# Where pieces of other work go beside an attention stream: a planner's rules and charges changed

## The chip, the cores and the metric

The kernel runs on one core of a Trainium2 chip. It uses all engines of that core: TensorE (PE in the profile) multiplies matrices, ScalarE (ACT) computes exponentials and tanh, VectorE (DVE) and GpSimd (POOL) do elementwise work, and SyncE (SP) issues most of the DMAs. The metric is the device time of one execution in microseconds. A single profiled execution gives the trace from which durations are read.

## The reference, cut to what matters

The input x has 4 images of 64 x 64 pixels with 128 channels, so 4096 tokens of 128 numbers in each of 4 batches. Two layers follow each other.

- Layer 0: ELU, two 3x3 convolutions, a gate `a * sigmoid(b)`, then causal attention with one head (queries and keys of 4 numbers, values of 16), whose result goes through W3 and is added to the gate's output and to x.
- Layer 1: a layer norm, attention with 16 heads of 8 numbers over all 4096 tokens of the image, a gated feed-forward network of 344 hidden units, another layer norm, and a mixture of 8 experts of which each token uses two.

```
scores = jnp.einsum('bqhd,bkhd->bhqk', q, k)        # 16 heads, 4096 x 4096 each
probs = jax.nn.softmax(scores.astype(jnp.float32), axis=-1)
attn = jnp.einsum('bhqk,bkhd->bqhd', probs, v)
h = x + attn @ wo
ffn = jax.nn.silu(h @ w1) * (h @ w3) @ w2
...
router_probs = jax.nn.softmax(x @ router_w + router_b, axis=-1)
top_p, top_i = jax.lax.top_k(router_probs, 2)
```

The 16-head attention dominates: 4 x 16 x 4096 x 4096 exponentials.

## The kernel before, in words

**The stream.** The 16-head attention of layer 1 is one long stream of rounds. Its unit is a segment: four heads (a group), 512 queries (a chunk) and all 32 key tiles of 128 keys. For one key tile a round does the following. TensorE computes the scores of the four heads into two PSUM tiles named `s` (four matmuls, each on 32 rows of the array), ScalarE takes the exponential of each `s` tile (128 x 1024) into a tile `e`, and TensorE later multiplies `e` with the values, summing into the PSUM tile `acc`. There are three `s` tiles, so TensorE can't compute scores much ahead of ScalarE. The value products trail the scores by a few rounds; they are kept in a list `undone` and issued in quarters of 128 queries (`add_values`).

**VectorE's tile.** In every full segment, key tile 20 isn't given to ScalarE. Class `Beside` gives its exponentials to VectorE: four units (one per head) each compute scores into the PSUM bank `m`, and VectorE evaluates a polynomial with nine instructions per unit (tiles `ey`, `em`, `eg`). When all four are done, two value halves (`half`, `acc<-ey` in the profile) add the tile to `acc`. The planner keeps its own estimate of when VectorE is done, `done_at`, and `can()` allows a half only when that time has come. Halves not placed by a segment's last value product are forced in there (`beside_rest`). So a segment has 31 rounds.

**Pieces.** All other work (the convolutions, the first attention's operands, the second attention's operands of the next batch, and the last part: output projection, feed-forward, router and experts of the batch at hand) is written as Python generators in the list `fillers`. Each `yield` ends a piece and names what it is taken to cost TensorE (mostly 0.46). Most pieces write into the one PSUM bank `m`, which VectorE then reads; `bank_held` says that a piece isn't finished with it, and `empty` that the bank is expected to be free. A round of the first attention (`first_step`) is put into the stream in the same way as a round of the second.

**The planner.** What is written in which place is decided while the program is built, in the `while True` loop at the end of `fast_path` (from line 1494). The order on every engine is the order as written (`InOrder`, L114 in the profile, which is why all instructions have that line). In each round the loop adds `EXPS` to a clock `turn_at`, writes one step's scores, and then has an account `left`: what is over of `EXPS` after the scores (`SCORES`) and the value quarters that must be done now (`VALUES` each), plus up to `AHEAD` from the round before. From this account it places, in this order: a piece that was held to go on, the jobs of VectorE's tile (`HEAD` for a unit, `PIECE` for a half), up to two pieces (`PIECE` each), and what value quarters still fit. `left` can be overdrawn: a job does so when it is late by its own list of due rounds, and a piece when the credit is high. The credit grows by `rate` per round (the work that is left divided by the rounds that are left, at least 40), shrinks by what is placed, and is at most 3.0. In batches 0 to 2 the pieces are the last parts of the batch and the preparation of the next one; in batch 3 they are only last parts. What isn't placed when the stream ends runs alone after it (`run_alone`).

Of the kernel before, what the change touches and what calls it, by code (L numbers as in the profile page):

```python
# [21 lines left out]
NQ = N // QB  # L22
# [5 lines left out]
NSLOT = P // SLOT  # L28
# [98 lines left out]
def fast_path(ctx: ExitStack, tc: tile.TileContext, a: dict, where: dict, out: bass.AP, verdict):  # L127
# [158 lines left out]
    steps_in, undone, fillers = [], [], []  # L286
    bank_held = [False]

    def do_step(step):
        scores, values, split = step  # L290
        undone.append([values, scores(), 4, split])

    def add_values(quarters):

        while quarters > 0:
            values, es, left, split = undone[0]
            some = min(left, quarters) if split else left
            values(es, *((4 - left, 4 - left + some) if split else ()))
            quarters -= some
            undone[0][2] -= some  # L300
            if some == left:
                undone.pop(0)

    def behind():
        return sum(step[2] for step in undone)

    def finish(leave):
        add_values(sum(step[2] for step in undone[: max(0, len(undone) - leave)]))
# [10 lines left out]
    def insert():  # L319

        while fillers:
            r = advance(fillers[0])
            if r is not None:
                return r[0]
            fillers.pop(0)
        return 0.0
# [510 lines left out]
    def second_operands_beside(b, st):  # L837

        while st.second < NQ:
            while len(st.ready) <= st.second or not folded[0]:  # L840
                if not alone[0]:
                    return
                yield 0.0, "wait"
            yield from second_operands(b, st)
# [208 lines left out]
    def beside_work(until, beside_pool=True):  # L1053
        while beside_todo and dve_at[0] + beside_todo[0][0] <= until:
            if not beside_pool and max(dve_at[0], turn_at[0] + 0.5) < pool_at[0]:
                break
            beside_todo.pop(0)[1]()
# [206 lines left out]
    batches = []  # L1264

    def run_alone(gens, until):

        gens, last = list(gens), {}
        while gens and not (until() and "rounds" not in last.values()):
            for gen in list(gens):  # L1270
                r = next(gen, None)
                while r is not None and r[1] == "held":
                    r = next(gen, None)
                last[gen] = r and r[1]
                if r is None:
                    gens.remove(gen)
                if steps_in:
                    do_step(steps_in.pop(0))
                    finish(1)
                elif undone:  # L1280
                    finish(0)
        while steps_in:
            do_step(steps_in.pop(0))
        finish(0)
        return gens
# [101 lines left out]
    now, quiet = [0], [False]  # L1387
# [75 lines left out]
    def fold_and_spread():  # L1463

        yield from spread(dve, taps1, wino1)
        pw = bank()
        pe.matmul(pw[:, :C], lhsT=once[:, :P], rhs=w3c[:, :C], start=True, stop=True)
        dve.tensor_copy(w3f[:, :C], pw[:, :C])
        pool.tensor_copy(w3f[:, C:], k_of["slot_row"])
        folded[0] = True  # L1470
        yield 0.0, "stop"
        yield from spread(dve, taps2a, wino2[:, :, :C], 0.5)

    def spread_beside():
        yield from spread(pool, taps2b, wino2[:, :, C:])
# [4 lines left out]
    left = run_alone(  # L1480
        [st.conv, first_attention(0, st), second_operands_beside(0, st), fold_and_spread(), spread_beside()],
        lambda: st.second >= plan[0].n and len(spread_of) == 3 and not st.plain,
    )
# [5 lines left out]
    credit, waiting = 0.0, False  # L1489


    EXPS, SCORES, VALUES, PIECE, HEAD, AHEAD = 1.81, 0.54, 0.218, 0.446, 0.23, 0.2
    ahead = 0.0
    while True:
        turn_at[0] += EXPS
        if steps_in:
            do_step(steps_in.pop(0))
        else:
            step = next(steps, False)
            if step is False:  # L1500
                break
            waiting = step is None
            if waiting:
                finish(0)
            else:
                do_step(step)
        b = now[0]
        if batches[b].second == NQ and len(batches) == b + 1 and b + 1 < B:
            Batch(b + 1)
            begun = 0  # L1510
            while begun < len(fillers) and (fillers[begun][2] in fetching or fillers[begun][2] is None):
                begun += 1
            fillers.insert(begun, [first_attention(b + 1, batches[b + 1]), PREPARE, None, False])

        rate = 1.0
        if batches[b].second == NQ:
            later = PREPARE * (B - len(batches)) + LAST * (last_parts_left[0] - 1)
            rate = (sum(part[1] for part in fillers) + later) / max(40, sum(steps_left) - 160)
        credit = min(3.0, credit + rate)
        must = max(0, behind() - 8)  # L1520
        left = ahead + EXPS - SCORES - VALUES * must
        took, beside = None, False
        if not quiet[0] and fillers and fillers[0][3] and not waiting:
            took = insert()
            credit -= took
            left -= took
        empty = bank_held[0] or bank_at[0] <= turn_at[0] + 0.3 or batches[b].second < NQ
        for job in jobs:
            cost = HEAD if job.units < NSLOT else PIECE
            if job.can() and empty and (left >= cost or job.late()):  # L1530
                if not (quiet[0] or bank_held[0] or steps_in or waiting):
                    job.piece()
                    left -= cost
                    beside = True
        for n in range(1 if waiting else 2):
            if took is None:
                go = waiting or not (quiet[0] or beside) and empty and credit > 0.0
                go = go and (waiting or left >= PIECE or credit > 1.5)
            else:
                go = took > 0.0 and bank_held[0] and left >= PIECE  # L1540
            if not go:
                break
            shift[0] = 0.0 if took is None else took
            took = insert()
            shift[0] = 0.0
            credit -= took
            left -= took
        add_values(must)
        while left >= VALUES and behind() > 6 and undone[0][3] and undone[0][3]():
            add_values(1)  # L1550
            left -= VALUES
        ahead = min(max(left, 0.0), AHEAD)
        for job in jobs:
            job.step()
        beside_work(turn_at[0] + 2.9, any(job.age > 3 * job.units + 4 for job in jobs if job.halves < 2))
# [681 lines left out]
def conv_attn_hybrid_kernel(tc: tile.TileContext, a: dict, where: dict, out: bass.AP):  # L2237
    nc = tc.nc
    with tc.tile_pool(name="verdict", bufs=1) as pool:
        verdict = pool.tile([1, 1], FP, name="verdict")  # L2240
        fast_path(tc, a, where, out, verdict)

        beyond = nc.values_load(verdict.bitcast(mybir.dt.int32))
        with tc.If(beyond > 0x3F800000):
            general_path(tc, a, where, out)
# [30 lines left out]
```

## Time and profile before

| what | us |
|---|---|
| median of 4 runs (7977.22 to 7985.18) | 7980.22 |
| the profiled execution, its own time | 7972.5 |
| its span, first to last instruction | 7970.7 |
| TensorE busy | 7755.9 (97%) |
| ScalarE busy | 7662.6 (96%) |
| VectorE busy | 4799.6 (60%) |
| 8256 exponentials `e<-s`, busy together | 7600.9 |
| ScalarE's longest wait in sum, `e` for `s` | 101.8 |

The stream begins at about 180 us, when the first layer of the first batch has gone far enough; 4123 of its rounds are written by the loop. By the start times of the exponentials batch 0 runs to about 2240 us, batch 1 to 4155, batch 2 to 6074 and batch 3 to 7914. After 7914 us the last part of the last chunk runs alone.

"Busy" of TensorE is a union of overlapping, modelled durations; it doesn't say that TensorE works at its peak. An idle time in a group's line is the time the engine stood still just before its instructions, with what ended it. A wait too short to leave an idle gap between overlapping instructions isn't in that column. Such a wait shows only in the distances between start times.

### The profile page before, as it was taken

The page shows a single profiled execution, that of the slowest core. Times are in us where ns is not written, and L with a number is a line of the kernel's source. Part 1 is how long each engine was busy: PE and PEld are TensorE (multiplying, and loading weights), DVE is VectorE, ACT ScalarE, POOL GpSimd, SP SyncE. Part 2 cuts the span into 40 slices and gives each one's busy share as a digit, 9 for nine tenths or more (in the row PEclk, how much of TensorE's full clock was granted, in tenths as well). Part 3 has the DMA queues.
Part 4 walks back from the last instruction along what each step waited for, and adds up shares of the span by engine and source line. Part 5 has one row for each costly group of instructions (what it writes and reads, how often), then busy time and mean ns, then how long its engine had stood idle before and what let it go on. Part 6 is the DMA issues. An engine that isn't in the chain of part 4 may idle for free.

```text
span 7970.7 us, 237947 instructions
## 1 busy us (share of the span) xinstructions
PE 7755.9 (97%) x103701; PEld 3277.6 (41%) x103701; DVE 4799.6 (60%) x9289; ACT 7662.6 (96%) x8459; POOL 671.6 (8%) x592
## 2 busy tenths in 40 slices
PE   7899999999999999999999999999999999999998
PEld 3333444444444444444444444444444333333334
DVE  4333556462666776666666777666666666666664
ACT  1899999999999999999999999999999999999996
POOL 1201211000022100000001210000000000000000
PEclk9999999999999999999999999999999999999998
DMA  2222011111110111111010011111111111111221
GB/s 73 67 68 69 23 61 33 61 40 53 35 34 15 50 39 52 38 29 43 25 41 29 19 43 43 51 42 35 32 29 53 50 49 52 51 54 50 70 73 38
DMA packets 334834, 360.96 MB, mean 45 GB/s; under 512 B 148211, under 2 KB 224467, under 8 KB 333779
## 3 DMA queue, kind: packets, MB, share of 16 engines
q1 hardware_dynamic: 329763, 343.87, 13.9%
q8 instruction: 814, 13.34, 0.7%
q10 hardware_dynamic: 4016, 1.77, 0.1%
q14 instruction: 241, 1.97, 0.1%
HBM read 209.50 MB, written 136.05 MB: 43 GB/s over the span
## 4 chain that ended last, share of the span: by engine, by line
PE 43%; issue 3%; DVE 2%; ACT 2%; DMA 0%; POOL 0%; SPq 0%; ACTq 0%; DVEq 0%; POOLq 0%
PE acc L114 22%; PE s L114 12%; PE m L114 9%; ACT e L114 1%; DVE ey L114 1%; DVE h L114 0%; DVE em L114 0%; DVE t L114 0%; DVE eg L114 0%; DVE by_e L114 0%; SPq L114 0%; DMA blocks<-d_y 0%; POOL rs L114 0%; POOL v L114 0%; POOL xt L114 0%
## 5 line engine op out<-in xcount | busy, mean ns | idle before, releaser
L114 ACT ACTIVATE e<-s 128x1024 f32<-128x1024 f32 x8256 | 7600.9, 1112 | 106.7 <-PE s L114 101.8
L114 PE MATMUL acc<-e,vg 128*9 128x128 f32 (+3 forms) x61880 | 4277.0, 387 | 1.9 <-DVE at L114 1.8
L114 PE MATMUL s<-qx,f_kx 32*128 32x512 f32 (+1 forms) x16512 | 2554.6, 496 | 86.4 <-ACT e L114 56.5
L114 PEld LDWEIGHTS acc<-e,vg 128*9 128x9 f32 x61880 | 1561.2, 90 | 1776.6 <-issue 1208.3
L114 PEld LDWEIGHTS s<-qx,f_kx 32*128 32x128 f32 (+1 forms) x16512 | 1048.1, 182 | 2066.5 <-ACT e L114 1338.7
L114 DVE SCALAR_TENSOR_TENSOR ey<-ey,eg 128x512 f32<-128x512 f32 x1344 | 941.0, 700 | 31.9
L114 DVE COPY at<-acc 128x512 f32<-128x512 f32 x131 | 90.6, 691 | 594.9 <-PE acc L114 590.5
L114 PE MATMUL m<-v,f_wino 128*32 128x256 f32 x5376 | 420.3, 391 | 12.1 <-POOL v L114 7.3
L114 DVE TENSOR_SCALAR ey<-m 128x512 f32<-128x512 f32 x448 | 307.7, 687 | 89.6 <-PE m L114 79.8
L114 DVE SCALAR_TENSOR_TENSOR eg<-em,ey 128x512 f32<-128x512 f32 x448 | 316.8, 707 | 11.4
L114 DVE SCALAR_TENSOR_TENSOR ey<-ey,em 128x512 f32<-128x512 f32 x448 | 316.7, 707 | 9.6
L114 POOL TENSOR_TENSOR rs<-ve,f_minus_half 128x4 f32<-128x4 f32 x64 | 65.3, 1020 | 3028.8 <-DVE ve L114 3028.8
L114 DVE SCALAR_TENSOR_TENSOR ey<-eg 128x512 f32<-128x512 f32 x448 | 312.9, 698 | 0.0
L114 POOL TENSOR_TENSOR v<-r 128x1024 f32<-128x1024 f32 x112 | 219.1, 1962 | 971.0 <-PE m L114 970.5
L114 DVE COPY sd<-m 128x512 f32<-128x512 f32 x168 | 116.0, 691 | 301.4 <-PE m L114 301.0
L114 PE MATMUL m<-f_we,y2T 128*32 128x256 f32 x3968 | 291.9, 388 | 0.0
L114 DVE TENSOR_TENSOR by_e<-m,gates 128x512 f32<-128x512 f32 x248 | 170.3, 687 | 176.6 <-PE m L114 175.4
L114 PE MATMUL m<-hT,f_fw 128*32 128x256 f32 (+1 forms) x2728 | 233.0, 390 | 1.3 <-DVE hT L114 1.1
L114 POOL TENSOR_TENSOR t<-t,h 128x512 f32<-128x512 f32 x32 | 44.5, 1391 | 2240.8 <-DVE h L114 2240.8
L114 DVE TENSOR_TENSOR t<-m,t 128x512 f32<-128x512 f32 x61 | 42.2, 692 | 308.8 <-PE m L114 308.7
L114 DVE TENSOR_SCALAR em<-ey 128x512 f32<-128x512 f32 x448 | 200.5, 447 | 13.7
L114 DVE TENSOR_SCALAR em<-em 128x512 int32<-128x512 int32 x448 | 196.2, 438 | 10.0
(260 smaller groups left out, 4380.0 us busy)
## 6 DMA issues: line engine op xcount, KB each, us to landing
f_kx<-d_k SPq DMA_DIRECT2D x139, 512.0 KB
qx<-d_q SPq DMA_DIRECT2D x152, 256.0 KB
d_q<-two SPq DMA_DIRECT2D x64, 512.0 KB
d_a<-at SPq DMA_DIRECT2D x128, 256.0 KB
vg<-d_v SPq DMA_DIRECT2D x32, 576.0 KB
d_k<-two SPq DMA_DIRECT2D x32, 512.0 KB
d_v<-vc SPq DMA_DIRECT2D x32, 288.0 KB
xe<-in_x_dram SPq DMA_DIRECT2D x32, 256.0 KB
```

What stands on the lines that cost most here:

```text
L114: made = op(*args, **kw)
```

## The change: rules and charges of the planner

The changed kernel computes the same with the same instructions. Only the loop's rules differ:

- `SCORES` goes from 0.54 to 0.55, `PIECE` from 0.446 to 0.456.
- A value half of VectorE's tile is placed when it can be and the account allows it (or it is late), outside the quiet rounds at a segment's start. It no longer asks for `empty`, nor that no piece holds the bank, nor that no step of the first attention waits. It no longer sets `beside`, so a piece may be placed in the same round. Units keep the old conditions.
- A new piece that finds too little in the account is placed when the credit is over 2.5 (before: over 1.5), or as long as the operands of the batch at hand aren't all prepared (`second < NQ`, which holds only early in batch 0).

```diff
-    EXPS, SCORES, VALUES, PIECE, HEAD, AHEAD = 1.81, 0.54, 0.218, 0.446, 0.23, 0.2
+    EXPS, SCORES, VALUES, PIECE, HEAD, AHEAD = 1.81, 0.55, 0.218, 0.456, 0.23, 0.2
...
         for job in jobs:
             cost = HEAD if job.units < NSLOT else PIECE
-            if job.can() and empty and (left >= cost or job.late()):
-                if not (quiet[0] or bank_held[0] or steps_in or waiting):
+            if job.can() and not (quiet[0] or waiting) and (left >= cost or job.late()):
+                if job.units == NSLOT:
+                    job.piece()
+                    left -= cost
+                elif empty and not (bank_held[0] or steps_in):
                     job.piece()
                     left -= cost
                     beside = True
         for n in range(1 if waiting else 2):
             if took is None:
                 go = waiting or not (quiet[0] or beside) and empty and credit > 0.0
-                go = go and (waiting or left >= PIECE or credit > 1.5)
+                go = go and (waiting or left >= PIECE or credit > 2.5 or batches[b].second < NQ)
             else:
```

## The prediction

> **What bounds it.** The page comes first, parts 1 and 5: which engines are full, and with what.
>
> ```profile
> PE 7755.9 (97%) x103701; PEld 3277.6 (41%) x103701; DVE 4799.6 (60%) x9289; ACT 7662.6 (96%) x8459; POOL 671.6 (8%) x592
> ...
> L114 ACT ACTIVATE e<-s 128x1024 f32<-128x1024 f32 x8256 | 7600.9, 1112 | 106.7 <-PE s L114 101.8
> ```
>
> ScalarE and TensorE are both nearly full. The exponentials overlap (1112 ns each, 7600.9 us for 8256), so their pace has to be read from start times in the trace: 4605 of the 8255 distances from one to the next lie between 900 and 910 ns. A round of the stream (two exponentials) therefore takes 1.809 us if ScalarE never waits. The other number needed is what a round costs TensorE, from the timeline of TensorE in two crowded rounds:
>
> ```profile
> 3008.46 0.51 PE L114 MATMUL s<-qx,f_kx 32*128 32x512 f32 x4
> 3008.90 0.64 PE L114 MATMUL m<-v,f_wino 128*32 128x256 f32 x8
> 3009.35 1.05 PE L114 MATMUL acc<-e,vg 128*9 128x384 f32 x16
> 3010.33 0.51 PE L114 MATMUL s<-qx,f_kx 32*128 32x512 f32 x4
> ```
>
> From start to start: scores 0.44, one piece 0.45, four value quarters 0.98, together 1.87 us, 0.06 more than ScalarE needs. Medians over all such neighbours in the trace: scores 0.44 plus 0.11 at the change back from values, so 0.55; a quarter 0.216; a piece 0.456, two in one round 0.887; a transposing piece 0.586; a unit of VectorE's tile 0.265; a value half of it 0.437. (The old charges 0.54 and 0.446 are below these, the new 0.55 and 0.456 agree.)
>
> Who is late is then read from the waits, ScalarE's for the last batch (from 6074 us to 7914) and then ScalarE's and TensorE's from 800 to 7914:
>
> ```profile
> ACT e L114 <- PE s L114: 1.7, 2, 1.2
> ...
> ACT e L114 <- PE s L114: 32.1, 43, 3.6
> ...
> PE acc L114 <- DVE ey L114: 11.5, 10, 2.1
> ```
>
> The visible waits are few. The rest of the loss is in rounds that are a few hundredths too long. Batch 3 shows it: 992 rounds times 1.809 are 1794.5 us, its 45 tanh and 16 router exponentials push the next exponential back by about 0.52 and 0.12, together 25 us, and it took 1848.8; 29 us are lost, 26.7 of them in rounds that lose under 0.3.
>
> An account explains that: charge every round, in the order in which TensorE's instructions are written, by the rows above; let what is left under 1.809 be carried to the next round up to a limit; sum what is over. With a limit of 0.07 us, one number fitted to four, it gives for batches 0 (from round 290), 1, 2 and 3: 12.7, 18.4, 20.7 and 28.3. The trace's rounds losing under 0.3 us sum to 12.3, 18.9, 21.4 and 26.7. So a round that is overfull costs its excess at once, and slack earlier does not pay for it.
>
> **Part 1: pieces and charges.** Up to round 289 both kernels place the same pieces. After it the same account on the changed order gives 10.1, 15.5, 19.8 and 38.8: 2.6, 2.9 and 0.9 less in batches 0 to 2, where the fuller charges leave fewer rounds over (1511 against 1595), and 10.5 more in batch 3. Batch 3 is worse for a reason that can be counted. Its credit stands at 3 almost throughout, so "credit > 2.5" still lets pieces in without room (215 against 191), and since a half of VectorE's tile no longer sets `beside`, a piece now enters the round of a half. A half, a piece and four quarters are 0.55 + 0.456 + 0.437 + 0.864 = 2.31 us, 0.50 over. In batch 3, 35 rounds hold both with three or four quarters and are over by more than 0.2, 15.1 us together; before has none. What follows a late round is the next scores on TensorE's queue, and behind them ScalarE. Sum 84.2 - 80.1 = +4. With the limit anywhere from 0 to 0.2 the sum moves between +1 and +14; I take +4, where the four batches of before fit.
>
> **Part 2: the end.** Before, the stream ends with only the bias product of the last part but one outstanding; its last 30 rounds hold four pieces. In the changed order batch 3 falls behind, and the router product, the eight expert products and the bias product of that part are left for after the stream, in front of the last part. The timeline of VectorE at the end has every duration:
>
> ```profile
> 7906.07 0.69 DVE L114 COPY at<-acc 128x512 f32<-128x512 f32 x1 [19.93 <-PE acc L114]
> 7911.10 0.55 DVE L114 RECIPROCAL sums<-sums 128x64 f32<-128x64 f32 x1 [3.27 <-DMA sums<-d_a]
> 7917.90 0.69 DVE L114 TENSOR_TENSOR an<-an,per 128x512 f32<-128x512 f32 x1 [6.25 <-DMA per<-d_r]
> 7943.52 0.69 DVE L114 COPY y2T<-s 128x512 f32<-128x512 f32 x1 [0.57 <-PE s L114]
> 7950.01 1.25 DVE L114 TENSOR_TENSOR by_e<-s,gates 128x512 f32<-128x512 f32 x2
> 7956.44 1.29 DVE L114 TENSOR_TENSOR by_e<-s,gates 128x512 f32<-128x512 f32 x2
> ```
>
> From the end of the copy to `an` are 11.1 us now, mostly DMAs. In the new VectorE order the copy is followed by y2T (7943.52 to the first expert 7950.01: 6.5), experts of two token tiles (7950.01 to 7956.44: 6.4), only then the reciprocal, then experts of the other two (6.4), then `an`. Reciprocal at 12.9 after the copy, `an` 6.8 later by the rows above, 19.7; the second experts end at 19.9 and set it. So 19.9 - 11.1 = +9. The DMAs of the last part lie under the experts, which is why not the whole 19 us is paid; should the blocks of y2T (written some 8 us before the stream ends; waits for them last up to 7.8) land late, it is up to 12.
>
> **Part 3: halves earlier.** A half needs the tile that VectorE finishes. The planner places it by its own estimate (`done_at`), and before it often waited further for `empty`. How a wrong estimate looks, on all engines:
>
> ```profile
> 2910.68 4.85 DVE L114 TENSOR_SCALAR h<-xt,mv,rs 128x128 f32<-128x128 f32 x4 [1.14 <-POOL rs L114]
> 2910.70 4.75 POOL L114 TENSOR_TENSOR r<-f_c_band 128x528 f32<-128x528 f32 x4
> ...
> 2922.79 0.38 PE L114 MATMUL acc<-ey,vg 128*9 128x256 f32 x1 [2.11 <-DVE ey L114]
> 2924.19 0.51 PE L114 MATMUL s<-qx,f_kx 32*128 32x512 f32 x4
> 2924.79 13.00 ACT L114 ACTIVATE e<-s 128x1024 f32<-128x1024 f32 x14 [2.44 <-PE s L114]
> ```
>
> The four normalisations take 4.85 us in place of 1.11 elsewhere (7941.84), because four GpSimd instructions run beside them; the tile is late, the half waits, the scores are queued behind it, ScalarE stands 2.44. In before 12 of 112 tiles delay their half, 18 us in all (some 20 on ScalarE). By the estimate's distance to the first half: under 0.5 us 15 tiles, waiting 0.51 on average; 0.5 to 1: 8, none waits; 1 to 1.5: 14, of which only the four behind such a collision wait, 2.6 each. The changed order has 28, 35 and 23, and three collisions close by. By these means 28 x 0.51 + 3 x 2.6 = 22, so +4; giving each new place the spread of lateness of the typical tiles of its batch gives about 15, so -3. I take +2, bounds -18 (all waits gone) and +21 (the 35 wait 0.5 as well). The 15 halves that before forced in at a segment's end become 3; they waited little (under 2 us in all), and that is inside these numbers.
>
> The row is a whole wait for each GpSimd instruction (4.85 beside 4.75). The Trainium skill, "SBUF — State Buffer", section "Who interferes with whom", has the rule that speaks against this part: a VectorE instruction of a two-port mode and a GpSimd one exclude each other for the whole instruction, the later one blocking fully. By it any SBUF-only step of VectorE's tile, not the normalisation alone, can lose a GpSimd instruction's length; at 1.2 us (an estimate from that page's rule and the row's 4.75/4) for each of the 28 closest tiles the half waits would be 34, not 20, and the sum 14 higher.
>
> Nothing else moves: GpSimd's order and the transfers on the queues are the same up to the end, and each next batch is prepared hundreds of rounds before it is needed.
>
> **Sum.** +4 + 9 + 2 = +15 us. The profiled execution took 7972.5 (span 7970.7), so it becomes 7987.5; the median of the timed runs stands 7.7 above it, so 7980.2 becomes 7995. That is +0.19%, just inside the 0.2% (16 us) under which I call two times the same.
>
> **Rivals.**
> 1. Halves wait much more (on the slower side): the 35 tiles at 0.5 to 1 us wait as the closest do. For it: nothing holds a half back any more, and VectorE's order shifts everywhere. Against: no half at that distance waited in before. 15 + 19 = +34, 8014; it decides from a mean wait of 0.1 us, which carries the sum over 16.
> 2. The waits for VectorE's tile go away (on the faster side), since halves no longer arrive in clusters. For it: two of the four collisions are no longer followed by a half. Against: three remain. 4 + 9 - 20 = -7, 7973; it makes the change faster from 15 us saved on.
> 3. The fuller charges also take away TensorE's other visible waits for VectorE (pieces waiting for their operands, some 18 us from 800 us on), 10 us of them, while batch 3 and the end lose as said: +5, 7985. Against: these waits are for VectorE's results, and the charges change only when pieces are placed, not what VectorE does.
>
> **Chances.** Forecast (7987 to 8003) 0.62, its own upper part above 7996 about half; rival 1 0.14; rival 2 0.1; rival 3 0.14. Slower by over 0.2%: 0.31 + 0.14 = 0.45. Faster by over 0.2% needs rival 2 with the end's 9 us gone too: 0.07. Same: 0.48. The range 7970 to 8014 takes in both rivals' own values; beyond it I see at most 2 in 10.
>
> **What would show it.** In batch 3 some 35 rounds with a half and a piece, each followed by exponentials 0.2 to 0.5 late, and the batch about 10 us longer (1859); batches 1 and 2 shorter by under 5; the distance from the last accumulator copy to `an` 20 us, not 11; TensorE's wait for `ey` near 12 us, three waits above 2. Wrong would be: the end as before, batch 3 not longer though its overfull rounds stand in the order (then ScalarE has slack that I deny), or waits for `ey` of 25 and more.

## The result, and the profile after

The changed kernel takes 7992.7 us (median of 40 runs, 7986.3 to 7998.5), the kernel before 7980.7 us (60 runs beside it). The ratio is 1.0015, with a 95% interval of 1.0011 to 1.0020: 12 us slower, inside the 0.2% that the prediction calls the same, and 2 us from the 7995 that it named. The profiled execution of the changed kernel took 7993.1 us, near its median. The one of before (7972.5) had been at the fast end of its runs, so both kernels were profiled once more (the runs again_before and again_after), and parts of the time are compared in two pairs.

A round is measured from its first exponential's start to the next round's. The last column runs from 1.81 us after the start of the last exponential to VectorE's last instruction.

| us | first 290 rounds | batch 0 after them | batch 1 | batch 2 | batch 3 | after the stream |
|---|---|---|---|---|---|---|
| before, two profiles | 593.6, 593.2 | 1458.4, 1458.0 | 1915.6, 1922.4 | 1918.6, 1919.4 | 1848.8, 1848.5 | 65.3, 66.3 |
| after, two profiles | 594.1, 590.2 | 1463.7, 1463.8 | 1909.0, 1908.5 | 1913.8, 1915.1 | 1865.1, 1865.1 | 75.3, 75.4 |
| mean difference | -1.3 | +5.6 | -10.3 | -4.6 | +16.5 | +9.6 |
| predicted | 0 | -2.6 | -2.9 | -0.9 | +10.5 | +9 |

(The halves' waits, +2 in the prediction, lie inside batches 0 to 2. The two pairs add up to +15.5, more than the 12 of the medians; the first profile of before ran 8 us under its median.) Part 1 of the changed kernel's page, and its costliest group:

```profile
PE 7787.2 (97%) x105013; PEld 3352.1 (42%) x105013; DVE 4798.6 (60%) x9289; ACT 7662.6 (96%) x8459; POOL 666.5 (8%) x592
...
L114 ACT ACTIVATE e<-s 128x1024 f32<-128x1024 f32 (+1 forms) x8256 | 7602.7, 1123 | 117.8 <-PE s L114 112.0
```

ScalarE does the same work in the same busy time. Its visible waits for scores grew from 101.8 to 112.0 us; this alone doesn't explain the difference. Where they grew is read from ScalarE's waits in batch 3 (6048 to 7916 us), and from the waits between 800 and 7930 us (in total, how many, the longest):

```profile
ACT e L114 <- PE s L114: 11.6, 25, 0.6
...
ACT e L114 <- PE s L114: 40.2, 55, 3.9
...
PE acc L114 <- DVE ey L114: 8.1, 7, 2.1
```

In batch 3 there were 2 such waits, 1.7 us together; now there are 25, none above 0.6 us. (By the starts of the exponentials this batch of the kernel before runs from 6055.6 to 7904.5 us, not from 6074 to 7914 as said ahead of the prediction; both waits lie in either window.) Waits for VectorE's tile (`ey`) did not grow: 8.1 us instead of 11.5. What stands in front of the small waits is seen in two neighbouring rounds of batch 3. TensorE's lines of the timeline:

```profile
7610.67 0.51 PE L114 MATMUL s<-qx,f_kx 32*128 32x512 f32 x4
7611.11 0.62 PE L114 MATMUL acc<-ey,vg 128*9 128x256 f32 x8
7611.66 0.64 PE L114 MATMUL m<-f_eb,g 8*32 8x128 f32 x16
7612.23 1.04 PE L114 MATMUL acc<-e,vg 128*9 128x512 f32 x8
7613.20 0.50 PE L114 MATMUL s<-qx,f_kx 32*128 32x512 f32 x4
```

and ScalarE's at that time:

```profile
7613.80 3.81 ACT L114 ACTIVATE e<-s 128x1024 f32<-128x1024 f32 x4 [0.59 <-PE s L114]
```

Scores, a half, a piece (the bias product) and four quarters, 2.53 us from scores to scores, where ScalarE needs 1.81; ScalarE then stands 0.59 us. Of the 36 rounds of batch 3 with a half and a piece, 35 hold three or four quarters. These 35, with the rounds right behind them, lost 19.4 us, and 26 of them are followed by a loss above 0.2. The kernel before has no such round.

The end, from VectorE's timeline:

```profile
7916.60 0.69 DVE L114 COPY at<-acc 128x512 f32<-128x512 f32 x1 [6.89 <-PE acc L114]
...
7917.35 0.71 DVE L114 STREAM_TRANSPOSE y2T<-blocks 128x512 f32<-128x512 f32 x1
...
7923.85 1.29 DVE L114 TENSOR_TENSOR by_e<-s,gates 128x512 f32<-128x512 f32 x2
...
7931.33 0.55 DVE L114 RECIPROCAL sums<-sums 128x64 f32<-128x64 f32 x1 [1.12 <-DMA sums<-d_a]
...
7938.38 0.69 DVE L114 TENSOR_TENSOR an<-an,per 128x512 f32<-128x512 f32 x1 [0.28 <-DMA per<-d_r]
```

Router and experts of the part before the last stand between the accumulator's copy and `an`: 21.1 us from the copy's end, where before had 11.1. This is the order of work that the prediction described.

Batch 0 holds what the prediction did not see, 4.1 us in one round. All engines there:

```profile
1118.59 4.82 DVE L114 TENSOR_SCALAR h<-xt,mv,rs 128x128 f32<-128x128 f32 x4 [1.14 <-POOL rs L114]
1118.61 4.71 POOL L114 TENSOR_TENSOR r<-f_c_band 128x528 f32<-128x528 f32 x4
...
1123.33 0.68 DVE L114 COPY at<-acc 128x512 f32<-128x512 f32 x1
...
1124.06 2.75 PE L114 MATMUL acc<-e,vg 128*9 128x512 f32 x24 [2.84 <-DVE at L114]
```

The collision of four normalisations with GpSimd's row sums, known from the kernel before, now has the accumulator's copy queued behind it instead of a half, and TensorE stands 2.84 us.

### The profile page after: what moved, and what is told of

The parts are those of the page before. It is cut to its first block, busy times and chain, and to the rows that moved or that the text cites. A ratio compares the mean times of both kernels' runs of the same rounds, so it can differ in the third digit from the quotient of the medians.

```text
span 7991.4 us, 240575 instructions
## 1 busy us (share of the span) xinstructions
PE 7787.2 (97%) x105013; PEld 3352.1 (42%) x105013; DVE 4798.6 (60%) x9289; ACT 7662.6 (96%) x8459; POOL 666.5 (8%) x592
## 5 line engine op out<-in xcount | busy, mean ns | idle before, releaser
L114 ACT ACTIVATE e<-s 128x1024 f32<-128x1024 f32 (+1 forms) x8256 | 7602.7, 1123 | 117.8 <-PE s L114 112.0
L114 PE MATMUL s<-qx,f_kx 32*128 32x512 f32 (+1 forms) x16512 | 2582.8, 495 | 87.6 <-ACT e L114 57.4
L114 PEld LDWEIGHTS acc<-e,vg 128*9 128x9 f32 x63288 | 1608.1, 90 | 1806.9 <-issue 1207.8
L114 PEld LDWEIGHTS s<-qx,f_kx 32*128 32x128 f32 (+1 forms) x16512 | 1078.1, 182 | 1992.2 <-ACT e L114 1214.4
L114 DVE TENSOR_SCALAR em<-ey 128x512 f32<-128x512 f32 x448 | 197.9, 442 | 13.1
```

Source lines behind the costliest of these rows:

```text
L114: made = op(*args, **kw)
```

## The experiments

What a round loses is its length less 1.809 us, less 0.52 for each tanh or first-layer activation in it and 0.12 for each router exponential. A round that loses 0.3 us or more is called a stall. "Overfull" is the prediction's account.

### One part at a time, and the sharing of rounds undone

e1_charges:

```diff
-    EXPS, SCORES, VALUES, PIECE, HEAD, AHEAD = 1.81, 0.54, 0.218, 0.446, 0.23, 0.2
+    EXPS, SCORES, VALUES, PIECE, HEAD, AHEAD = 1.81, 0.55, 0.218, 0.456, 0.23, 0.2
```

> The kernel before with the new charges alone (SCORES 0.55, PIECE 0.456). Three theories are kept apart in all four runs of this set. The account: what a version costs is the time by which rounds are overfull (a lead of at most 0.07 us carried, 1.809 us a round) and the work left behind the stream. Behind only: the batches cancel, and the 12 us between the two kernels are the nine router and expert products left at the end. Accidents: any new order of the same work moves the time by up to 10 us either way, through stalls that happen to meet, and nothing follows from the rounds. Here the account gives 74.6 us overfull where the kernel before has 80.1 (batches 10.4, 15.5, 19.6, 29.1 against 12.7, 18.4, 20.7, 28.3), and about four products more are left behind the stream, some 2 us: -3.5 us, ratio 0.9996. Behind only: +2 us, 1.0002. No piece shares a round with a half of VectorE's tile, so the waits for these halves stay near the 20 us of before.

e2_halves, on the kernel before:

```diff
-            if job.can() and empty and (left >= cost or job.late()):
-                if not (quiet[0] or bank_held[0] or steps_in or waiting):
+            if job.can() and not (quiet[0] or waiting) and (left >= cost or job.late()):
+                if job.units == NSLOT:
+                    job.piece()
+                    left -= cost
+                elif empty and not (bank_held[0] or steps_in):
```

> The kernel before with the new rule for the halves alone (a half asks neither for a free bank nor for no piece begun, and a piece may share its round); the old charges, pieces without lead at a credit over 1.5. Nothing more than before is left behind the stream. The account gives 99.0 us overfull against 80.1 (batches 12.0, 22.4, 26.3, 38.3; 81 rounds with a half and a piece): +19 us, ratio 1.0024, of which batch 1 has 4, batch 2 has 6, batch 3 has 10. Behind only: 0 us, 1.0000. If the halves' earlier places were what costs, their waits for VectorE would grow above 20 us; if these waits shrink, at most -18 us off the +19.

e3_credit, on the kernel before:

```diff
-                go = go and (waiting or left >= PIECE or credit > 1.5)
+                go = go and (waiting or left >= PIECE or credit > 2.5 or batches[b].second < NQ)
```

> The kernel before with the new credit rule alone (a piece without lead only at a credit over 2.5, or while the batch's second operands are still made). The account gives 76.2 us overfull against 80.1 (batches 12.6, 18.5, 18.8, 26.3), and the last chunk's router, expert and bias products stay behind the stream as in the changed kernel: -4 and +9, together +5 us, ratio 1.0006, the copy of the last accumulator to the last normalised tile 20 us instead of 11. Behind only: +9 us, 1.0011.

e4_beside, on the changed kernel:

```diff
                 if job.units == NSLOT:
                     job.piece()
                     left -= cost
+                    beside = True
```

> The changed kernel, but a half of VectorE's tile again keeps a new piece out of its round; its other new freedoms and the other two parts stay. The account gives 66.3 us overfull against 84.2 in the changed kernel and 80.1 before (batches 9.6, 14.1, 15.4, 27.2): batch 3 some 11 us shorter than in the changed kernel. But the pieces pushed out of these rounds stay behind: about twice as much as in the changed kernel, some 18 us after the stream instead of 9. Together +4 us on the kernel before, ratio 1.0005, 8 us under the changed kernel's 1.0015. Behind only: +18 us, 1.0023.

| run | ratio to before (95%) | batch 0 | batch 1 | batch 2 | batch 3 | after the stream |
|---|---|---|---|---|---|---|
| e1_charges | 0.9998 (0.9989 to 1.0007) | 1457.2 | 1917.0 | 1917.9 | 1849.0 | 67.0 |
| e2_halves | 1.0024 (1.0014 to 1.0034) | 1455.4 | 1924.8 | 1925.1 | 1860.1 | 66.4 |
| e3_credit | 1.0013 (1.0004 to 1.0022) | 1459.1 | 1918.5 | 1921.9 | 1849.3 | 75.3 |
| e4_beside | 1.0021 (1.0012 to 1.0030) | 1459.2 | 1909.5 | 1906.3 | 1859.1 | 94.4 |

What follows:

- **The halves' new rule alone makes batch 3 longer, by 11.4 us** (31 rounds with a half and a piece, 11.6 us lost there). The total of +20 us met the account's +19, but partly by luck: batch 1 holds one stall of 7.9 us where the two profiles of before lose 2.6 and 5.3 us in that place, batch 2 one of 5.0 (2.8 and 4.3 before). So the account's +4 and +6 for these batches aren't shown, batch 3's +10 is.
- **The credit rule alone makes the end longer**: 75.3 us after the stream, from the copy's end to `an` 19.7 us; the changed kernel has 75.3 and 21.1. Each batch differs by under 3 us from the nearer profile of before, which is less than one profile can tell. Where the account does look, it was borne out: the rounds that lose under 0.3 us sum to 12.3, 18.7, 18.6 and 24.6 us, 5 less than before (12.3, 18.9, 21.4, 26.7), most of it in batches 2 and 3 as worked out. But stalls took it back: 24.7 us in batch 2 against 17.6 and 18.8 before, and in batch 3 ten of them (3.9 us) against two (2.3).
- **The charges alone do nothing measurable.** The account promised 2 to 3 us in batch 0 and in batch 1. The rounds that lose under 0.3 us sum to 13.0, 19.0, 21.8 and 27.6 us, against 12.3, 18.9, 21.4 and 26.7 before.
- **Undoing the sharing shows what it had been paid with.** In batch 3 e4_beside has no half with a piece, and the batch is 6 us shorter than in the changed kernel, not 11. The work left behind the stream grows to 94.4 us, 19 more than in the changed kernel where 9 more were expected. "Behind only", with +18 us, came nearer than the account with +4.

Most of what batch 3 of e4_beside fell short of the 11 us is in new waits: TensorE waited there for `y2T` six times, 6.4 us in all (twice, 2.4 us, in the kernel before). One of them, which cost its round 2.8 us, in the timeline of all engines:

```profile
7609.74 2.78 SPq L114 DMA_DIRECT2D blocks<-d_y  x4
...
7616.22 0.71 DVE L114 STREAM_TRANSPOSE y2T<-blocks 128x512 f32<-128x512 f32 x1 [2.89 <-DMA blocks<-d_y]
...
7616.98 0.43 PE L114 MATMUL m<-y2T,f_rw 128*32 128x128 f32 x8 [1.89 <-DVE y2T L114]
```

The transposed tile's DMAs were issued at 7609.7 and landed for VectorE at 7616.2; the planner had put the product that needs it too close behind.

### Is the halves' waiting a cost of its own?

A half may come only 5.0 us after the account has VectorE done; e5_before_later on the kernel before, e6_after_later on the changed one:

```diff
-            return self.halves < 2 and self.ready == NSLOT and self.done_at <= turn_at[0] + 0.4
+            return self.halves < 2 and self.ready == NSLOT and self.done_at <= turn_at[0] - 5.0
```

> The kernel before, but a half may only be placed 5.0 us after the time at which the account has VectorE done with its tile, where the kernel before allows it from 0.4 us ahead of that time. It prices the halves' waits alone: 13 of the 112 tiles held TensorE in the kernel before, and ScalarE lost 22.7 us in the rounds around them. If these waits are a cost of their own, they go and nothing takes their place: account 77.3 us overfull against 80.1 and 20 us of waits less, together -23 us, ratio 0.9971, nothing more left behind the stream. If the lateness of VectorE that they show holds TensorE elsewhere anyway (at the accumulator's copy, at a bank), the time stays at -3 us, 0.9996, and the waits reappear under other names.

> The changed kernel with the same 5.0 us margin for the halves. Account 84.9 us overfull against 84.2, the end unchanged (about 10 us longer than before). If the halves' waits are a cost of their own, the 19.6 us that ScalarE lost around 13 tiles in the changed kernel go: ratio 1.0015 less 0.0023, 0.9992. If they only move, 1.0015.

| run | ratio to before (95%) | batch 0 | batch 1 | batch 2 | batch 3 | after the stream |
|---|---|---|---|---|---|---|
| e5_before_later | 1.0002 (0.9993 to 1.0011) | 1457.4 | 1915.0 | 1913.7 | 1860.2 | 68.1 |
| e6_after_later | 1.0024 (1.0014 to 1.0034) | 1459.7 | 1913.0 | 1918.8 | 1863.0 | 75.5 |

The expectation of -23 us failed, though the waits for `ey` are gone: neither run's list of waits from 800 to 7900 us has one for TensorE's matmuls. In e5_before_later batches 0 to 2 are 6 us shorter than in the one profile of before and 14 shorter than in the other; batch 3 is 11.5 longer and takes it back. There the two late halves now stand at a segment's end, where the accumulator must be copied before the next segment's values. The timeline in batch 3, all engines:

```profile
7738.41 1.05 PE L114 MATMUL acc<-ey,vg 128*9 128x256 f32 x16
...
7740.39 0.69 DVE L114 COPY at<-acc 128x512 f32<-128x512 f32 x1 [6.44 <-PE acc L114]
...
7740.86 2.88 ACT L114 ACTIVATE e<-s 128x1024 f32<-128x1024 f32 x3 [0.17 <-PE s L114]
7741.14 0.12 PEld L114 LDWEIGHTS acc<-e,vg 128*9 128x9 f32 x8 [0.29 <-DVE at L114]
```

Fifteen rounds like this one, 62 apart, lose 0.31 to 0.39 us each. Fifteen others, with a unit of VectorE's tile beside their value products, lose 0.36 to 0.46 each, where no such round of the kernel before loses as much as 0.25. Together these thirty lose 10.9 us, nearly all of the 11.5. So the waits do cost, but a later place is not free.

e6_after_later lost 6 us on the changed kernel instead of gaining 18. Its batch 2 holds the same stall that e2_halves has in batch 1. All engines:

```profile
4231.26 6.34 DVE L114 SCALAR_TENSOR_TENSOR ey<-ey,eg 128x512 f32<-128x512 f32 x3
...
4232.49 8.95 POOL L114 TENSOR_TENSOR v<-r 128x1024 f32<-128x1024 f32 x4
...
4237.52 2.14 DVE L114 TENSOR_SCALAR pos<-xe 128x512 f32<-128x512 f32 x1
...
4242.04 1.12 PE L114 MATMUL m<-f_consts,pos 128*128 128x128 f32 x4 [6.92 <-DVE pos L114]
```

Three steps of VectorE's tile take 6.34 us (2.15 where GpSimd is idle), `pos` 2.14 instead of 0.41, and TensorE stands 6.92 us: a placement that costs 7.9 us, with the same 6.92 us of waiting in e2_halves. The total of a single version can't be read more finely than such a stall.

### The same kernels again

Each kernel unchanged, for how far a profile repeats.

> The kernel before once more, unchanged, for how far one profiled execution repeats: ratio 1.0000. If the stalls follow from the order of the work, each batch repeats within 2 us of 1458.4 (from round 290), 1915.6, 1918.6 and 1848.8 us, and the rounds that lose over 1 us are the same ones. If they are accidents of the execution, batches differ by 5 us or more.

> The changed kernel once more, unchanged: ratio 1.0015. If the stalls follow from the order of the work, its batches repeat within 2 us of 1463.7, 1909.0, 1913.8 and 1865.1 us, with the 4.1 us stall in batch 0 where the accumulator's copy waits behind four slow normalisations, and its end is again 10 us longer than before.

Ratios 1.0001 (0.9991 to 1.0011) and 1.0014 (1.0004 to 1.0024); the batches stand in the first table. From round 290 on all repeat within 2 us but one: batch 1 of before, 6.8 us apart. (The first 290 rounds of the changed kernel are 3.9 us apart.) Its stalls lie in the same rounds, but are larger: 3.88 and 1.39 instead of 2.52 and 0.05 in two neighbouring rounds, 4.51 instead of 3.07, 4.07 instead of 2.81. So where the stalls stand follows from the order of the work, but their size is in part an accident of the execution: a step of 1.3 to 1.4 us, at the first place 2.7, comes with each or doesn't. TensorE's granted clock goes with it: in the second profile it fell to 0.50 in batch 1 at 2314, 2666, 2925 and 3973 us, in the first not once. The section on the hardware has more.

### Taking the collision away

The edit, on the kernel before (e7_before_hold), on the changed kernel (e8_after_hold) and on e1_charges (e9_charges_hold):

```diff
         h = chunk("h")
         layernorm(t, h)
+        if not alone[0]:
+            planned = pool_at[0]
+            pool.tensor_copy(small("hold", [1]), h[:, QB - 1 :])
+            pool_at[0] = planned
```

The planner's clock for GpSimd is put back, so every other instruction keeps its place.

> The kernel before in its own order, with one more instruction for GpSimd after each normalisation of h: it copies one column of h, so that GpSimd's four row sums begin behind h instead of beside it. It tests whether the six places where the normalisation takes 4.85 us instead of 2.15 are what stops TensorE, under whatever name. If they are: these six come to 2.2 us, the rounds in the 22 us behind them no longer lose the 17.1 us that they lost in the profile of before (22.9 in its second profile), TensorE's idle stretches of 2 us near 1396, 2662, 2921, 4656 and 4903 us go, and with them some of the stretches at clock 0.50 that follow them: -16 us, ratio 0.9980 (0.9972 to 0.9985). If VectorE is late there for other reasons, or GpSimd's later sums hold up the products that wait for them: 0 us, 1.0000.

> The changed kernel in its own order with the same instruction. 17.8 us were lost behind the six slow normalisations in its profile (18.5 in its second), the 4.1 us stall in batch 0 among them: -16 us on the changed kernel, ratio 0.9995 to the kernel before. What remains over the kernel before with the same instruction must be the change alone, without the accident in batch 0: batch 3's +16 and the end's +10, less what batches 1 and 2 give: between +12 and +17 us, 0.0015 to 0.0021. If the normalisations are not the cause, 1.0015.

> The kernel before with the new charges alone and the same instruction: the account's best of the single parts (74.6 us overfull against 80.1, some 2 us more behind the stream), with 17.4 us lost behind slow normalisations in the profile of the new charges alone. If both hold, -1.4 as measured without the instruction and -16: ratio 0.9978. If the instruction does nothing, 0.9998.

| run | ratio to before (95%) | batch 0 | batch 1 | batch 2 | batch 3 | after the stream |
|---|---|---|---|---|---|---|
| e7_before_hold | 0.9993 (0.9984 to 1.0002) | 1456.8 | 1920.5 | 1918.4 | 1848.9 | 65.7 |
| e8_after_hold | 1.0006 (0.9997 to 1.0015) | 1456.3 | 1906.0 | 1914.1 | 1865.2 | 76.3 |
| e9_charges_hold | 0.9991 (0.9982 to 1.0000) | 1454.8 | 1913.9 | 1919.5 | 1849.0 | 68.2 |

Every normalisation of h in the stream now takes 1.11 or 1.12 us. Of the expected 16 us only 5.6 to 7.2 came, by the ratios. In the changed kernel the batch 0 stall is gone, in the same round (timeline of e8_after_hold, all engines):

```profile
1115.90 1.11 DVE L114 TENSOR_SCALAR h<-xt,mv,rs 128x128 f32<-128x128 f32 x4 [1.14 <-POOL rs L114]
...
1117.31 0.69 DVE L114 COPY at<-acc 128x512 f32<-128x512 f32 x1 [0.29 <-PE acc L114]
1117.31 4.73 POOL L114 TENSOR_TENSOR r<-f_c_band 128x528 f32<-128x528 f32 x4
```

This settles batch 0: 1463.7 becomes 1456.3. Where VectorE's tile is under way, the collision only moves on to its steps (e7_before_hold, all engines):

```profile
1384.00 6.32 POOL L114 TENSOR_TENSOR r<-f_c_band 128x528 f32<-128x528 f32 x4
...
1386.40 1.21 DVE L114 TENSOR_SCALAR em<-ey 128x512 f32<-128x512 f32 x1
...
1394.16 0.38 PE L114 MATMUL acc<-ey,vg 128*9 128x256 f32 x1 [1.95 <-DVE ey L114]
```

`em` takes 1.21 us instead of 0.43, GpSimd's four sums 6.32 instead of 4.73, and the half still waits 1.95. Behind the six places 17.6 us were lost in this profile, as much as before (17.1 and 22.9); in e8_after_hold 9.3 instead of 17.8, in e9_charges_hold 12.9 instead of 17.4. The gain of e7_before_hold is itself not certain, its interval reaches over 1.

With the instruction on both sides, the change costs 10.7 us by the medians (7984.1 against 7973.5), a little under the 12 to 17 expected: by the profiles -0.5 in batch 0, -14.5 and -4.3 in batches 1 and 2, +16.3 in batch 3 and +10.6 after the stream, 7.6 together; the other 4 us of the two profiles' difference lie ahead of batch 0's round 290.

### A version that beats both

e10_three is e9_charges_hold with a margin for the halves, but not in batch 3:

```diff
-            return self.halves < 2 and self.ready == NSLOT and self.done_at <= turn_at[0] + 0.4
+            return self.halves < 2 and self.ready == NSLOT and self.done_at <= turn_at[0] + (0.4 if now[0] == B - 1 else -3.0)
```

> Three edits that each gained or lost little are put together: the kernel before with the new charges, with GpSimd's instruction behind each normalisation of h, and with halves held back until 3.0 us after the account has VectorE done, but only in batches 0 to 2, since in batch 3 the wider margin cost 11 us. In the run with the first two edits, seven halves still held TensorE, by 10.9 us together. Account 73.9 us overfull against 74.6 without the margin. If these waits go for good, -11 us on the run with two edits (0.9991): ratio 0.9977. If two thirds of them return elsewhere, as with the wider margin on the kernel before (6.5 us of 20 kept in batches 0 to 2), -4 us: 0.9986. If all return, 0.9991.

7959.0 us, ratio 0.9973 (0.9962 to 0.9984): 23 us faster than the kernel before beside it, slightly better than what was expected if the waits go for good (0.9977). Batches 1453.1, 1904.9, 1915.2, 1849.1, and 66.8 after the stream. TensorE's value products wait for `ey` only once, 0.2 us, and ScalarE's waits from 800 to 7930 us are little more than half of those of e9_charges_hold (31.1 us, 26 waits):

```profile
ACT e L114 <- PE s L114: 17.6, 19, 3.5
```

## Why the prediction held, step by step

The total was right (+15 forecast, +12 measured), but its terms were right only in part, and that their errors cancelled was luck: batch 0 and batch 3 cost more than forecast, batches 1 and 2 less.

- **Part 2, the end: right.** +9 forecast, +10.0 and +9.1 in two pairs, and e3_credit shows that the credit rule alone brings it. The path from the copy to `an` took 21.1 us instead of the 19.9 worked out; the sum lacked the reciprocal's wait of 1.12 us for its DMA, and so the reciprocal's path, not the second experts, set it.
- **Part 1, batch 3: the mechanism right, the size too small.** The 35 rounds are there, 26 with a loss behind them above 0.2 us. The term was "15.1 us together over"; the rounds lost 19.4, and the batch grew by 16.5 instead of 10.5. In the rounds shown above, the half took 0.55 us before its piece (0.437 in the sum) and the bias product 0.57 (0.456).
- **Part 1, batches 0 to 2: the step that failed.** "2.6, 2.9 and 0.9 less ... where the fuller charges leave fewer rounds over" rested on an account whose limit was fitted to the kernel before. In the rounds losing under 0.3 us, the kind that the account was fitted to, nothing was gained: 12.3, 20.3 and 21.9 us against 12.3, 18.9 and 21.4. Alone, too, the charges gained nothing there. The credit rule alone did bring the 4 us worked out for it in these rounds (5 by the profile), but not in the changed kernel.
- **What took its place** are stalls of 0.3 us and more. Batch 0 gained one of 4.1 us (shown by e8_after_hold to be the collision). In batches 1 and 2 such stalls fell from 18.5 and 17.6 us (25.5 and 18.8 in the second profile) to 10.7 and 13.7 (10.8 and 14.9). TensorE's waits show where: in batch 1 its waits for VectorE other than those for `ey` fell from 10.9 us (in both profiles) to 1.9 and 1.3; behind the four slow normalisations of batches 1 and 2 the kernel before lost 13.1 and 17.3 us, the changed one 8.8 and 9.5 (three of the four were followed by a half that waited, now two are). No part alone shortens batch 1 or 2 to this, while e4_beside (1909.5, 1906.3) does, so at least two of the parts are needed together. Which, and why, is not settled: no run has two of them without the third.
- **Part 3: right in size.** Near 12 us of waiting and three waits above 2 were forecast; there were 8.1 us, in three long waits (2.1 and twice 1.9) and four short ones. ScalarE lost 19.6 us around the 13 delayed tiles, 22.7 before: -3 where +2 was taken. The trouble with GpSimd, read from one row as a risk for halves, was the right one: all three long waits follow a normalisation of 4.8 us. But it also struck, unforeseen, at the accumulator's copy.
- **The rivals.** Rival 1 fell: of the 13 delayed tiles none stood at the distance it named. Rival 2 fell: three long waits remain. Rival 3 is the one whose effect partly came true: from 800 us to the stream's end TensorE's waits for VectorE other than those for `ey` fell from 20.2 and 20.1 us to 12.1 and 11.6, where it said 10 less. But its cause did not: with the fuller charges alone (e1_charges) these waits are 21.2 us.

## What to carry to other kernels

In a stream that two engines fill to 97%, a rule that lets two extra things share a round is paid in most of these rounds (26 of 35 here), while work that a rule defers is paid at the end: count both, per batch. A planner's clock for one engine must know what the engine beside it does to it; here GpSimd's row sums ran beside VectorE's normalisations, and made them last 4.85 us, six times in each version without the extra instruction. Before a change of 0.1% is read part by part, profile the same kernel twice.

## What the runs showed of the hardware

**A short stand of TensorE can cost a second time.** The same stall in two executions of the kernel before: TensorE waits 2.10 and 2.09 us for `ey`. The windows after it (length, busy time and count of PE, PEld, DVE, ACT and POOL, granted clock, DMA share, GB/s) in the first profile:

```profile
1398.00:1399.00 1.00, 0.79 (x22) 0.55 (x23) 0.27 (x2) 0.00 (x0) 0.00 (x0) 1.00 0.30 46
1399.00:1400.00 1.00, 1.00 (x19) 0.46 (x7) 0.59 (x1) 0.00 (x0) 0.00 (x0) 1.00 0.00 0
```

and in again_before:

```profile
1396.00:1397.00 1.00, 0.84 (x12) 0.31 (x16) 0.24 (x2) 0.00 (x0) 0.00 (x0) 0.50 0.31 47
1397.00:1398.00 1.00, 1.00 (x19) 0.60 (x12) 0.57 (x1) 0.00 (x0) 0.00 (x0) 0.50 0.00 0
1398.00:1399.00 1.00, 1.00 (x12) 0.47 (x6) 0.00 (x0) 0.00 (x0) 0.00 (x0) 0.50 0.00 0
```

The granted clock stays at 1.00 in the one and falls to 0.50 in the other, and the round loses 2.81 and 4.28 us. Over all 14 profiles, 70 stands of TensorE of 1.8 to 3.1 us lie between 840 and 7900 us: 48 had a stretch at clock 0.50 begin by 3 us after their end, of 3.4 us as a rule, 22 had none. The six rounds around a stand lost 4.35 us on average with it (mean stand 2.25) and 2.78 without (mean 2.10). Of 62 stands of 0.7 to 1.2 us, 5 had one. Much of the scatter between executions of one kernel can be this. The Trainium skill, "TensorE: Matmul & The Clock Gate", section "What's actually happening", has a free-running window of about 3.4 us behind the half clock, which agrees with the stretch's length and with a stand that is followed by it only sometimes; its section "Why this matters for your kernels" warns of gaps above about 3 us, and here stands of 2 us were enough in two of three cases.

**GpSimd slows more of VectorE than the normalisation.** `em` (a tensor_scalar, one input) went from 0.43 to 1.21 us, three steps on `ey` and `eg` (two inputs) from 2.15 to 6.34, `pos` from 0.41 to 2.14, each beside GpSimd's sums. The Trainium skill, "SBUF — State Buffer", section "Who interferes with whom", names both kinds, and these runs agree. By that page whoever issues first blocks the other for its whole instruction. Here both were slowed: GpSimd's four sums took 6.32 us instead of 4.73.
